# A mixture of experts behind cross attention: which freed memory the first tiles of the expert stage are put in

## The chip, the core and the metric

The kernel runs on one core of a Trainium2 chip. The metric is the device time of one execution in microseconds (us). The engines are TensorE (PE in the profile), VectorE (DVE), ScalarE (ACT), GpSimd (POOL) and SyncE (SP), which here only issues DMAs. Lines such as L1551 are lines of the kernel before.

## The reference

`x` has 16 blocks of 128 rows of 512. Attention over a small context is added to it, and then the output of a routed feed-forward layer with 32 experts, 8 of them for each row, and one shared expert:

```python
x = x + xattn(layernorm(x), ctx, ctx)
h = layernorm(x)
tidx, tw = gate(h)                       # 8 of 32 experts for each row, with weights
comb = zeros(T, 32).at[rows, tidx].set(tw)
g, u = h @ w1[e].T, h @ w3[e].T          # for each expert e
routed = sum over e of comb[:, e] * ((silu(g) * u) @ w2[e].T)
sh = (silu(h @ sw1.T) * (h @ sw3.T)) @ sw2.T
x = x + routed + sh
```

## The kernel before

**Stages.** Attention comes first (to about 105 us), then the routing (`route`, `slot_tokens`: which row goes to which slot of which expert), to about 183 us. Beside the routing and for some 28 us after it TensorE works on the shared expert. Its last step is `shared_down` (L1381): two matmuls per block of 128 rows fill a PSUM bank `y`, and `add_down` (L1395) has VectorE add `y` to the block `xs[b]` (here called the sum of x; L1396) and SP write the block to `out` (L1397). From about 211 us on the 32 experts follow one after another, each in two pieces of at most 352 rows.

**An expert's work.** `gather` fetches the rows of 128 slots (POOL issues it), `transpose` (VectorE) and `block_copies` (small copies, most on ScalarE, some on VectorE, L1506) turn them into `xall`, whose parts are called `half`. The first and the last expert go through `direct` and `up` (L1533): a matmul with w1, silu on ScalarE into a tile `sg` (L1551), a matmul with w3, and a product on VectorE into `sa` (L1555). All others go through `seven` (L1624), which forms the up-projection of two halves with seven products instead of eight. It needs sums of quarters of the weights (`weight_sums`, L1563: four VectorE instructions s1, s2, a21 in place, s4, all at L1574) and of the tokens (`token_sums`, L1592: t1, t2, b12 in place, t4, at L1603). Its first product is copied by ScalarE from PSUM into a tile `p1` (L1661), and VectorE adds further products to it, in tiles `u2` and `z` (L1622). `down` (L1740) multiplies `sa` with the expert's w2, `evict` (L1763) scales the result by the routing's weight into a tile `yw` on ScalarE, and `send` scatters it with adding into `out` (POOL, L1721).

**Order.** The instructions of TensorE, VectorE, ScalarE and POOL stand in the order in which the program text issues them; no scheduler moves them. `soon(f)` puts an evacuation one step later. Within the experts' loop, side work (`on_DVE`, `on_ACT`: sums, transposes, copies) is dealt out over the steps of a piece by a count of its cost. Weight sums for expert k+1 are issued in the first piece of expert k, token sums for k+1 in its second.

**Memory.** Tiles come from pools. When a pool is closed, later pools may take its memory, and the first instruction that writes there waits for all that last used it. Two such changes of hands matter:

- `early` holds the routing's tiles. It is closed at L1424, and `tp` (L1427) is opened behind it. `tp` holds `own`, `blocks` and, in the kernel before, `yw` (4 tiles of 2 KiB per partition).
- `x_only` holds the rows of x (`xs`). It is closed at L1814, after the last sums of x have been issued, and `late` (L1815) takes its memory. `late` holds `sg` (3 tiles of 2 KiB), `s1`, `s2`, `s4` (2 each of 2 KiB), `t1`, `t2`, `t4`, `p1`, `u2` and `z`.

The loop that issues the last eight blocks of the shared expert reads as follows (`products` holds the sum of x):

```python
for i, b in enumerate(downs):            # L1806
    shared_down(b, ps_p)
    transpose_to(min(6 + i, last_slice(3)))
    ...                                  # some copies into xall
    for f in products:
        f()
    products.clear()
x_only.close()                           # L1814
late = ctx.enter_context(tc.tile_pool(name="late", bufs=2, side="right"))
```

Of the kernel before, what the change touches and what calls it, by code (L numbers as in the profile page):

```python
# [9 lines left out]
F32 = mybir.dt.float32  # L10
# [8 lines left out]
P = 128  # L19
# [27 lines left out]
def tile_xattn_moe(  # L47
# [16 lines left out]
    B, S, D = x.shape  # L64
# [5 lines left out]
    TB = 512  # L70
# [981 lines left out]
    def experts(ups, in_order, later, products):  # L1052
# [374 lines left out]
        tp = ctx.enter_context(tc.tile_pool(name="tp", bufs=2))  # L1427
# [15 lines left out]
        def experts_at(j):  # L1443

            for k in range(E):
                a, b = max(begins[k], j * P), min(begins[k + 1], (j + 1) * P)
                if a < b:
                    yield k, a - j * P, b - j * P, a - begins[k]
# [5 lines left out]
        xg, yws = {}, {}  # L1454
# [75 lines left out]
        def soon(f, after=1):  # L1530
            jobs.setdefault(now + after, []).append(f)

        def up(n, i, w, banks):  # L1533

            k, first, end = pieces[n]
            m = min(end, begins[k] + ROOM[ORDER[k]]) - first
            act = acts_of[k % NA][:, :, first - begins[k] : first - begins[k] + m]

            acc = banks[w] = ps_p.tile([P, TB], F32, tag="p", name="gu")
            for d in range(ND):  # L1540
                nc.tensor.matmul(
                    acc[:, 0:m],
                    lhsT=wup[k % NW][:, w, d, ts(i, P)],
                    rhs=half[n % NH][:, d, 0:m],
                    start=(d == 0),
                    stop=(d == ND - 1),
                )
            if w == 0:
                sl = late.tile([P, 2, M], F32, tag="sg", name="sg", bufs=3)
                sl = banks[2] = sl.rearrange("p a b -> p (a b)")  # L1550
                soon(lambda: nc.scalar.activation(sl[:, 0:m], acc[:, 0:m], AF.Silu))  # L1551
            else:
                sl = banks[2]
                soon(
                    lambda: nc.vector.tensor_tensor(  # L1555
                        act[:, i, :], sl[:, 0:m], acc[:, 0:m], ALU.mult
                    )
                )

        M = TB // 2  # L1560
        sums = {}

        def weight_sums(k):  # L1563


            a11, a12, a21, a22 = (
                wup[k % NW][:, :, d : d + 2, ts(i, P)] for i in range(2) for d in (0, 2)
            )
            s1, s2, s4 = (
                late.tile([P, 2, 2, P], F32, tag=name, name=name) for name in ("s1", "s2", "s4")  # L1570
            )
            sums[k] = s1, s2, a21, s4
            return [
                lambda o=o, a=a, b=b, op=op: nc.vector.tensor_tensor(o, a, b, op)  # L1574
                for o, a, b, op in (
                    (s1, a21, a22, ALU.add),
                    (s2, s1, a11, ALU.subtract),
                    (a21, a11, a21, ALU.subtract),
                    (s4, a12, s2, ALU.subtract),
                )  # L1580
            ]

        def halves_of(k):

            h = ROOM[ORDER[k]] // 2
            return [
                half[n % NH][:, d : d + 2, 0:h] for d in (0, 2) for n in (2 * k, 2 * k + 1)
            ]
# [32 lines left out]
        def add(out_, a, b):  # L1621
            soon(lambda: nc.vector.tensor_tensor(out_, a, b, ALU.add))  # L1622

        def seven(k):  # L1624


            h = ROOM[ORDER[k]] // 2
            act = acts_of[k % NA]
            a11, a12, _, a22 = (
                wup[k % NW][:, :, d : d + 2, ts(i, P)] for i in range(2) for d in (0, 2)  # L1630
            )
            s1, s2, s3, s4 = sums[k]
            b11, _, b21, b22 = halves_of(k)
            t1, t2, t3, t4 = tsums.pop(k)
            both = 2 * h <= TB
            size = M if both else HM

            def new(name, n, size, bufs=2):
                t = late.tile([P, 4 * M if name == "z" else TB], F32, tag=name, name=name, bufs=bufs)
                return t[:, 0 : n * size].rearrange("p (n t) -> p n t", n=n)[:, :, 0:h]  # L1640

            def silu(to, of, after):
                soon(lambda: nc.scalar.activation(to, of, AF.Silu), after)

            def times(to, a, b, after):
                soon(lambda: nc.vector.tensor_tensor(to, a, b, ALU.mult), after)

            act0, act1 = act[:, 0, 0:h], act[:, 1, 0:h]
            act2 = act[:, :, h : 2 * h]

            for w in (slice(0, 2),) if both else (slice(0, 1), slice(1, 2)):

                many = w.stop - w.start

                def bank():
                    p = ps_p.tile([P, TB], F32, tag="p", name="p")
                    return p[:, 0 : many * size].rearrange("p (n t) -> p n t", n=many)[:, :, 0:h]

                pa, p1 = bank(), new("p1", many, size, 1)
                product(pa, a11[:, w], b11)  # L1660
                soon(lambda p1=p1, pa=pa: nc.scalar.copy(p1, pa))  # L1661
                yield
                pb, u2 = bank(), new("u2", many, size)
                product(pb, s2[:, w], t2)
                add(u2, p1, pb)
                yield
                pc = bank()
                z = new("z", 2 * many, size)
                z0, z1 = z[:, 0:many], z[:, many : 2 * many]
                product(pc, s1[:, w], t1)  # L1670
                add(z1, u2, pc)
                yield
                pd = bank()
                product(pd, s3[:, w], t3)
                add(z1, z1, pd)
                yield
                product(pa, a12[:, w], b21, first=False)
                if both:
                    sl = new("sg", 1, TB, 3)[:, 0]
                    silu(sl, pa[:, 0], 1)  # L1680
                    times(act0, sl, pa[:, 1], 2)
                elif w.start == 0:
                    silu(act0, pa[:, 0], 1)
                else:
                    times(act0, act0, pa[:, 0], 1)
                yield
                product(pc, s4[:, w], b22, first=False)
                add(z0, u2, pc)
                if both:
                    sl = new("sg", 2, M, 3)  # L1690
                    silu(sl, z[:, 0::2], 2)
                    times(act2, sl, z[:, 1::2], 3)
                elif w.start == 0:
                    silu(act2, z, 2)
                else:
                    times(act2, act2, z, 2)
                yield
                product(pd, a22[:, w], t4, first=False)
                add(u2, u2, pd)
                if both:  # L1700
                    sl = new("sg", 1, TB, 3)[:, 0]
                    silu(sl, u2[:, 0], 2)
                    times(act1, sl, u2[:, 1], 3)
                elif w.start == 0:
                    silu(act1, u2[:, 0], 2)
                else:
                    times(act1, act1, u2[:, 0], 2)
                yield
# [52 lines left out]
            soon(lambda: evict(j, y))  # L1761

        def evict(j, y):  # L1763
            yws[j] = tp.tile([P, D], F32, tag="yw", name="yw", bufs=4)
            nc.scalar.activation(yws[j], y, AF.Copy, scale=wt[:, j : j + 1])  # L1765
            for args in waiting:
                send(*args)
            waiting.clear()
            rows_of = {k: (a, b) for k, a, b, _ in experts_at(j)}
            ks = sorted(rows_of)  # L1770
            send(j, ks[0], *rows_of[ks[0]])
            waiting.extend((j, k, *rows_of[k]) for k in ks[1:])
# [33 lines left out]
        for i, b in enumerate(downs):  # L1806
            shared_down(b, ps_p)
            transpose_to(min(6 + i, last_slice(3)))
            for f in copies[len(copies) * i // len(downs) : len(copies) * (i + 1) // len(downs)]:
                f()  # L1810
            for f in products:
                f()
            products.clear()
        x_only.close()  # L1814
        late = ctx.enter_context(tc.tile_pool(name="late", bufs=2, side="right"))  # L1815
        KEPT = 2

        def fast(k):
            return 0 < k < E - 1
# [14 lines left out]
        for n in range(len(pieces)):  # L1834
            k = pieces[n][0]
            odd = n % 2
# [8 lines left out]
                steps = 4  # L1845

            on_DVE, on_ACT = [], []
            if not odd and fast(k + 1):
                on_DVE += [(4, f) for f in weight_sums(k + 1)]
            to_turn = last_slice(min(n + 4, last_piece))  # L1850
            turning = [(5, lambda j=j: transpose(j)) for j in range(n_turned, to_turn)]
# [29 lines left out]
            for step in range(steps):  # L1881
# [3 lines left out]
                for i, (side, total) in enumerate(sides):  # L1885
                    due = done / sum(dues)
                    while side and lefts[i] > total * (1 - due) + 0.01:
                        c, f = side.pop(0)
# [97 lines left out]
```

## Time and profile before

| what | value |
|---|---|
| median of 3 runs | 879.42 us (879.39 to 880.23) |
| profiled execution: time, and its span from first to last instruction | 881.58 us, 879.7 us |
| granted TensorE clock, mean | 0.998 |
| TensorE busy, 211 to 225 us / 225 to 240 / 240 to 255 | 14.00 / 11.08 / 15.00 us |
| ScalarE busy in the same | 8.03 / 14.46 / 14.53 us |
| VectorE busy in the same | 10.65 / 13.09 / 13.16 us |
| TensorE busy in each stage of 60 us from 300 to 840 | 60.00 us |

The first three columns of time are the last step of the shared expert's sums with expert 0 (211 to 225), the first half of expert 1 (225 to 240) and what follows. A busy figure of a stage cannot tell what the stage waits for; for that the waits, the chain of waits and the timeline of each engine are read. A row of the waits has the engine and line that waited, what it waited for, the total in us, how often, and the longest. A row of a timeline has start, length, engine, line, operation, output and inputs, shapes and count, and in brackets the idle time before it and what ended it.

### The profile page before, as it was taken

Reading aid. Unit: us, or ns where it says so; the run is one execution under the profiler, and the core shown is the slowest. Engines: PE = TensorE matmul, PEld = TensorE weight load, DVE = VectorE, ACT = ScalarE, POOL = GpSimd, SP = SyncE. Lnnn points to the kernel's source line nnn. Section 1 sums busy time; section 2 is a strip of 40 time slices with the busy share of each in tenths; the row PEclk is TensorE's granted clock in tenths of the full one; section 3 lists DMA queues with packets and bytes.
Section 4 is the critical chain, followed back from the end, with each engine's and each line's share of the span. In section 5 each row is a group of like instructions: output and inputs, shape, how many; then the busy total and the mean of one; then the engine's idle time right before and its main releaser. Section 6 shows DMA issues by size and latency. Waiting matters only on the chain.

```text
span 879.7 us, 13628 instructions
## 1 busy us (share of the span) xinstructions
PE 861.7 (98%) x4015; PEld 538.5 (61%) x4015; DVE 625.9 (71%) x1599; ACT 689.4 (78%) x1570; POOL 476.4 (54%) x590
## 2 busy tenths in 40 slices
PE   8999999999899999999999999999999999999995
PEld 5344444546565665666666666676767777777763
DVE  7877778846976777777777777776867777777510
ACT  5888732537998898888898989898898899999831
POOL 4487550053355576656556666565556656554454
PEclk9999999999999999999999999999999999999999
DMA  9111112556377788778778787877778888786544
GB/s 307 58 48 50 49 50 77 211 156 197 110 169 162 172 202 191 177 169 182 165 181 184 192 188 191 186 210 175 187 158 206 195 176 178 197 190 122 88 76 54
DMA packets 59876, 137.15 MB, mean 156 GB/s; under 512 B 12168, under 2 KB 16392, under 8 KB 59792
## 3 DMA queue, kind: packets, MB, share of 16 engines
q0 software_dynamic: 32032, 69.25, 41.9%
q1 hardware_dynamic: 27680, 66.81, 22.1%
q8 instruction: 34, 0.56, 0.3%
q14 instruction: 50, 0.41, 0.2%
q10 hardware_dynamic: 80, 0.13, 0.0%
HBM read 96.71 MB, written 46.73 MB: 163 GB/s over the span
## 4 chain that ended last, share of the span: by engine, by line
PE 88%; POOL 3%; ACT 3%; issue 2%; DVE 2%; DMA 2%; POOLq 0%; ACTq 0%
PE p L1612 42%; PE y L1749 24%; PE gu L282 6%; PE sc L489 5%; PE oT L505 4%; PE x L459 2%; PE y L1386 2%; POOL out_dram L1721 2%; ACT xall L1506 2%; DMA out_dram<-yw,token 1%; PE tok L1038 1%; DVE x L1396 1%; PE lgT L566 0%; PE lg L581 0%; DVE xall L1506 0%
## 5 line engine op out<-in xcount | busy, mean ns | idle before, releaser
L1506 ACT COPY xall<-blocks 32x256 f32<-32x256 f32 (+10 forms) x1137 | 418.9, 368 | 15.0
L1721 POOL DMA_INDIRECT out_dram<-yw,token x150 | 246.2, 1641 | 212.0 <-ACT yw L1765 79.7
L1749 PE MATMUL y<-wdn,sa 128*128 128x512 f32 (+2 forms) x672 | 259.1, 594 | 0.0
L1460 POOL DMA_INDIRECT xgs<-rows,token x138 | 150.7, 1092 | 134.5 <-DVE token L1050 53.2
L1612 PE MATMUL p<-xall,wup 128*128 128x270 f32 (+27 forms) x720 | 185.6, 394 | 2.0 <-ACT p L1661 2.0
L1612 PEld LDWEIGHTS p<-xall,wup 128*128 128x128 f32 x720 | 136.5, 190 | 46.6 <-issue 16.1
L1749 PEld LDWEIGHTS y<-wdn,sa 128*128 128x128 f32 (+2 forms) x672 | 100.9, 171 | 83.7 <-issue 72.2
L1765 ACT ACTIVATE yw<-y,wt 128x512 f32<-128x512 f32 x138 | 94.7, 686 | 70.6 <-PE y L1749 39.4
L1612 PE MATMUL p<-t,s 128*128 128x270 f32 (+27 forms) x480 | 125.7, 394 | 1.1 <-DVE t L1603 1.1
L1612 PEld LDWEIGHTS p<-t,s 128*128 128x128 f32 x480 | 91.0, 190 | 39.0 <-issue 22.4
L1509 DVE STREAM_TRANSPOSE blocks<-xgs 128x512 f32<-128x512 f32 x138 | 97.5, 706 | 0.2
L1622 DVE TENSOR_TENSOR z<-u,p 128x270 f32<-128x270 f32 (+27 forms) x96 | 48.8, 509 | 68.5 <-PE p L1612 63.3
L499 ACT ACTIVATE p<-sc 128x1024 f32<-128x1024 f32 x64 | 62.1, 1023 | 13.6 <-PE sc L489 13.6
L1612 PE MATMUL p<-t,wup 128*128 128x270 f32 (+27 forms) x240 | 63.8, 396 | 0.7 <-DVE z L1622 0.7
L1612 PE MATMUL p<-xall,s 128*128 128x270 f32 (+27 forms) x240 | 63.6, 396 | 0.5 <-DVE z L1622 0.4
L1612 PEld LDWEIGHTS p<-t,wup 128*128 128x128 f32 x240 | 45.0, 190 | 25.9 <-issue 14.1
L282 PE MATMUL gu<-xall,sup 128*128 128x512 f32 x128 | 59.2, 601 | 0.0
L1622 DVE TENSOR_TENSOR u<-u,p 128x270 f32<-128x270 f32 (+27 forms) x48 | 24.4, 509 | 44.9 <-PE p L1612 36.9
L1612 PEld LDWEIGHTS p<-xall,s 128*128 128x128 f32 x240 | 45.2, 190 | 16.9 <-issue 4.3
L1506 DVE COPY xall<-blocks 32x256 f32<-32x256 f32 (+11 forms) x187 | 51.3, 299 | 3.5
L489 PE MATMUL sc<-qT,kz 32*128 32x512 f32 x256 | 44.2, 639 | 0.5 <-DVE qT L480 0.2
L1603 DVE TENSOR_TENSOR t<-xall,t 128x540 f32<-128x540 f32 (+27 forms) x60 | 43.3, 722 | 0.5
(218 smaller groups left out, 916.2 us busy)
## 6 DMA issues: line engine op xcount, KB each, us to landing
wup<-in_w_dram SPq DMA_DIRECT2D x64, 512.0 KB
wdn<-in_w_dram SPq DMA_DIRECT2D x32, 512.0 KB
rows<-xn SPq DMA_DIRECT2D x16, 256.0 KB
out_dram<-x SPq DMA_DIRECT2D x16, 256.0 KB
x<-in_x_dram SPq DMA_DIRECT2D x15, 256.0 KB
out_dram<-yw,token POOLq DMA_INDIRECT x150
xgs<-rows,token POOLq DMA_INDIRECT x138
cTs<-in_cT_dram SPq DMA_DIRECT2D x4, 256.0 KB
```

What stands on the lines that cost most here:

```text
L282: nc.tensor.matmul(acc, lhsT=sup[:, w, d, ts(i, P)], rhs=xnT[k][:, d, :], start=(d == 0), stop=(d == ND - 1),)
L489: nc.tensor.matmul(scs[j // 2][:, j % 2], lhsT=kzs[b // 4 % 2][rows, b % 4, i, :], rhs=qT[rows], start=True, stop=True, tile_position=(j * ...
L499: nc.scalar.activation(p, sc, AF.Exp, scale=1.0 / HD**0.5)
L1460: nc.gpsimd.indirect_dma_start(out=t, out_offset=None, in_=rows[:, :], in_offset=bass.IndirectOffsetOnAxis(ap=token[:, j : j + 1], axis=0) ...
L1506: yield on_ACT, 1 + many, lambda dst=dst, of=of, copy=copy: copy(dst, of)
L1509: nc.vector.transpose(blocks[:, j % NB_BUF, :], xgs[:, j % NG_BUF, 0:D])
L1603: yield lambda o=out_, a=a, b=b: nc.vector.tensor_tensor(o, a, b, ALU.subtract)
L1612: nc.tensor.matmul(acc[:, i, 0:h], lhsT=w[:, i, d, :], rhs=x[:, d, :], start=(first and i == d == 0), stop=(i == outs[-1] and d == 1), ski ...
L1622: soon(lambda: nc.vector.tensor_tensor(out_, a, b, ALU.add))
L1721: ins = nc.gpsimd.indirect_dma_start(out=flat, out_offset=bass.IndirectOffsetOnAxis(ap=token2[:, k - 1 : k] if a else token[0:b, j : j + 1 ...
L1749: nc.tensor.matmul(y[c0:c1, :], lhsT=acts_of[k % NA][:, i, col : col + c1 - c0], rhs=wdn[k % NW][:, i, :], start=(i == 0), stop=(i == NI - 1),
L1765: nc.scalar.activation(yws[j], y, AF.Copy, scale=wt[:, j : j + 1])
```

## The change

It has four parts. The tiles `sg` are taken from `tp` instead of `late`, both in `up` and in `seven`, and so are `s1`, `s2` and `s4`. The tiles `yw` go the other way, from `tp` to `late`. The weight sums of expert 1 are issued in the loop over the last blocks of the shared expert, in its first pass, ahead of the sum of x; the experts' loop leaves them out for its first piece. The number of instructions on each engine stays the same, and no size changes.

```diff
@@ up
             if w == 0:
-                sl = late.tile([P, 2, M], F32, tag="sg", name="sg", bufs=3)
-                sl = banks[2] = sl.rearrange("p a b -> p (a b)")
+                sl = banks[2] = tp.tile([P, TB], F32, tag="sg", name="sg", bufs=3)
                 soon(lambda: nc.scalar.activation(sl[:, 0:m], acc[:, 0:m], AF.Silu))
@@ weight_sums
             s1, s2, s4 = (
-                late.tile([P, 2, 2, P], F32, tag=name, name=name) for name in ("s1", "s2", "s4")
+                tp.tile([P, 2, 2, P], F32, tag=name, name=name) for name in ("s1", "s2", "s4")
             )
@@ seven
             def new(name, n, size, bufs=2):
-                t = late.tile([P, 4 * M if name == "z" else TB], F32, tag=name, name=name, bufs=bufs)
+                pool = tp if name == "sg" else late
+                t = pool.tile([P, 4 * M if name == "z" else TB], F32, tag=name, name=name, bufs=bufs)
@@ evict
-            yws[j] = tp.tile([P, D], F32, tag="yw", name="yw", bufs=4)
+            yws[j] = late.tile([P, D], F32, tag="yw", name="yw", bufs=4)
@@ the loop over the last blocks of the shared expert
-            for f in products:
+            for f in (weight_sums(1) if i == 0 else []) + products:
                 f()
             products.clear()
@@ the experts' loop
-            if not odd and fast(k + 1):
+            if not odd and k and fast(k + 1):
                 on_DVE += [(4, f) for f in weight_sums(k + 1)]
```

## The prediction

> **What bounds the kernel now.** I read the page first, then the waits of the stretch from 205 to 246 us, the chain of waits there, and the order of TensorE's and VectorE's instructions in time. TensorE is busy nearly all the time and carries the chain, so only time in which TensorE stands still can be won.
>
> ```profile
> PE 861.7 (98%) x4015; PEld 538.5 (61%) x4015; DVE 625.9 (71%) x1599; ACT 689.4 (78%) x1570; POOL 476.4 (54%) x590
> PE 88%; POOL 3%; ACT 3%; issue 2%; DVE 2%; DMA 2%; POOLq 0%; ACTq 0%
> ```
>
> The change touches two waits, both on the write-outs of x. They are the first two lines here; the last three are TensorE's own waits a little later:
>
> ```profile
> ACT sg L1551 <- DMA out_dram<-x: 5.7, 1, 5.7
> DVE s L1574 <- DMA out_dram<-x: 3.0, 1, 3.0
> PE p L1612 <- ACT p L1661: 2.0, 1, 2.0
> PE p L1612 <- DVE t L1603: 1.1, 1, 1.1
> PE p L1612 <- DVE z L1622: 0.7, 1, 0.7
> ```
>
> A wait of ScalarE costs nothing by itself. The chain (start, length, what) shows that this one does:
>
> ```profile
> 214.97 0.70 DVE x L1396
> 215.69 2.85 DMA out_dram<-x
> 218.65 0.38 ACT sg L1551
> ...
> 234.36 0.46 ACT p L1661
> 234.84 0.52 DVE u L1622
> ...
> 237.29 0.71 DVE blocks L1509
> 238.14 0.45 DVE z L1622
> 238.63 6.18 PE p L1612 x20
> ```
>
> From the last sum of x the chain goes through its transfer to the first silu. ScalarE then works without a pause (copies into xall, silus) until the copy of p at 234.36, VectorE follows, and TensorE is let go at 238.63. So 5.7 us of waiting on ScalarE reach TensorE 16 us later. What they cost is read from TensorE's starts (start, busy, operation):
>
> ```profile
> 227.36 2.63 PE L1612 MATMUL p<-t,s 128*128 128x352 f32 x8 [1.09 <-DVE t L1603]
> 229.83 1.35 PE L1612 MATMUL p<-xall,wup 128*128 128x352 f32 x4
> 231.02 1.88 PE L1749 MATMUL y<-wdn,sa 128*128 128x512 f32 x4
> 234.86 1.45 PE L1612 MATMUL p<-xall,wup 128*128 128x352 f32 x4 [1.97 <-ACT p L1661]
> 236.46 1.45 PE L1612 MATMUL p<-xall,s 128*128 128x352 f32 x4
> 238.63 1.45 PE L1612 MATMUL p<-t,wup 128*128 128x352 f32 x4 [0.73 <-DVE z L1622]
> 239.92 1.35 PE L1612 MATMUL p<-xall,wup 128*128 128x352 f32 x4
> 241.10 2.53 PE L1612 MATMUL p<-t,s 128*128 128x352 f32 x8
> ```
>
> These are the seven products of expert 1's first half, which begin at 224.93. One product takes 1.18 us from start to start (239.92 to 241.10), a group of y 1.72 (chain). Seven and one y: 7 x 1.18 + 1.72 = 9.98 us. The round takes 239.92 - 224.93 = 14.99. **So 5.0 us are lost here**; the three listed waits add up to only 3.8, because they are counted from modelled ends of matmuls.
>
> **What the Trainium skill says.** Perfetto Trace Analysis, section "Tensor Engine Instruction (MATMUL, LD_WEIGHTS)": TensorE's end times are an estimate, and ScalarE and VectorE are strict first-in-first-out. The trace agrees with both: 5.0 us by starts against 3.8 by ends, and VectorE's matmul-independent copies stand behind its 3.0 us wait. The same page, "DMA Instruction — HWDGE (DVE, Sync)": a DMA's semaphore comes only after its write is confirmed, which can be surprisingly late for HBM; here 2.85 us pass from issue to release. VectorE: DVE Perf Modes, "The TRN2 errata": an fp32 tensor_tensor over 512 elements takes 691 ns; the trace's s rows take 681 to 693. SBUF — State Buffer, "SBUF: two separate sides": VectorE with two SBUF inputs and a GpSimd operation that reads SBUF lock each other out. The second expert's weight sums ran at 231.93 beside a gather (231.58 to 232.58) in 0.68 and 0.69 us, so I charge nothing.
>
> **The change, part by part.**
> (a) *sg from the routing's memory.* The instruction order of the changed kernel shows that the first silu waits for TensorE alone. Its matmuls are a quarter of the first piece's 7 us after 211.11, so ready at about 212.9; ScalarE's copies end at 198.91 + 14.05 = 212.96. It starts at about 213.05 instead of 218.65: **ScalarE is 5.6 us earlier.** The wait for x's eight queues moves to the first copy of p on ScalarE (p1 stays in the rows' memory), due near 228.9, when the transfers have long landed (218.54): free.
>
> (b) *Weight sums of expert 1 ahead of the last eight sums of x.* Four instructions of 0.69 us, starting about 0.6 to 0.7 apart: 2.6 us taken from the stretch after 215.7 and put behind the copies that end at 199.6. There VectorE idles now:
>
> ```profile
> 199.02 0.57 DVE L1506 COPY xall<-blocks 32x256 f32<-32x256 f32 x2
> 203.16 0.69 DVE L1396 TENSOR_TENSOR x<-y,x 128x512 f32<-128x512 f32 x1 [3.57 <-PE y L1386]
> ```
>
> 2.6 fit in 3.57. Their operands are there: the loads were issued before 153.4. Odd is that y's four matmuls (from 197.38, 0.43 apart) end near 199.1, four us before that sum starts; why its release came late the trace doesn't tell. If the release is as late again, the sums hide wholly. If it comes at once, the sums of x start at 202.2, 0.96 us earlier than now. If VectorE stops for the 3.57 us whatever is queued, everything behind comes 2.6 us later. I take the first; -0.96 and +2.6 are the ends.
>
> (c) *VectorE after 215.66.* The 3.0 us wait goes, and 2.6 of sums: it moves to the token sums' t1, the first user of the rows' memory there. In the new order: three copies (1.1) to 216.8, transpose and own (0.8) to 217.6, product sa (0.42), transpose and own to 218.85, sa, two copies to 219.9. t1 needs ScalarE's three copies behind the second silu: 213.05 + 0.4 + 4.42 + 0.4 + 1.56 = 219.9. So t1 starts at about 219.95 instead of 225.49, over 1 us after the last landing. t2 ends at 221.8; TensorE wants it at 226.11: the 1.1 us stall is gone.
>
> (d) *TensorE's round.* With no stall its products start at 224.93, 226.11, 227.3, 228.5, y at 229.7, then 231.4 (needs p1's copy), 232.6 (needs z's first sum) and 233.7 (needs z's second). ScalarE: third silu by 222.35, nine copies (3.3), fourth silu by 226.1, seven copies (2.75), p1's copy ends at 229.35. VectorE: u at 229.4, s4 0.65, z to 230.95, copies, transpose and own, second z to 233.15. Slacks 2.0, 1.6 and 0.6 us: **all 5.0 us go.**
>
> (e) *yw into the rows' memory.* The first eviction, now at 238.23, comes 15 us after the landing; four buffers as before: nothing. SP's loads keep their order; the one for expert 4 loses a wait on VectorE that did not end last. POOL's order is unchanged; its gathers hang on VectorE's transposes, which come no later, and the scatters on evictions that move forward.
>
> (f) *Afterwards.* ScalarE has no pause over 0.1 us until 276.6, so its 5.6 us of lead stay while TensorE gains 5.0; the stall at 267.95 (0.55 by starts, 0.38 listed, behind p1's copy) can shrink by up to 0.55. I take 0.2. Later nothing holds TensorE but its own work, so the gain stands to the end.
>
> **Sum:** 5.0 + 0.2 = 5.2 us. The profiled execution had a span of 879.7 and 881.58 in all, which would be 876.4; the runs' median is 879.42, 2.2 less, so the forecast is 879.42 - 5.2 = **874.2**. Its own range is 873.5 (all of the later stall, x earlier) to 875.6 (slacks 1 us worse).
>
> **Rivals.**
> *A, the weight sums push x (2.6 us later).* ScalarE's copies from 204.76 on read transposes that start right behind a sum of x, and would stand 2.3 us; t1 would wait for a landing at 221.2 and VectorE's own queue to about 222.5. First z then ends at about 233.3 against 232.55, second at 235.5: stalls of 0.75 and 1.0, so the gain is 3.2: 876.2. For it: the odd 3.57 us. Against: the label says PE.
> *B, lost banks: slower.* The sums of x also empty y's PSUM banks. The third (10th row block) ends at 207.65, and TensorE takes its bank at 211.11; the other margins are 3.3 us or more. If the four instructions delay x by d, TensorE loses d - 3.3. To lose more than the 5.0 it needs d over 8.3; at d = 11, 882. Against: 2.6 us of work with operands that are there, so d could exceed 2.6 only by a wait nobody shows.
> *C, hardly a gain.* ScalarE's lead is eaten before p1's copy (silus waiting on TensorE, copies on transposes), or TensorE meets a later limit and gives it back: 878.5. Against: every later stage of 60 us up to 840 has TensorE busy 60.0. *The change not doing what it says* is excluded by the order: sg waits for TensorE alone.
>
> **How the numbers follow.** Forecast 0.80, A 0.10, C 0.06, B 0.04. Range 873.4 to 877.2: the forecast's ends with 0.1 below, and A with 1 us of spread above (the three runs differ by 0.84). A measurement tells about 0.2% (1.76 us, that is 877.66) from no change. Faster: forecast and A, less a little, 0.89; same 0.06; slower 0.05.
>
> **What would show it.** The first sg at about 213 with no DMA wait; the four weight sums at 199.6 and sums of x not after 203.2; t1 near 220; TensorE's first round 10 us instead of 15, with no wait on p1 or t. It is wrong if the sums of x start after 205, if p1's copy comes after 231, or if TensorE's gain at 240 is not there at 840.

## The result, and the profile after

The changed kernel takes 875.97 us (median of 6 runs, 875.87 to 876.05) beside 879.78 us for the kernel before in the same comparison (6 runs, 879.23 to 880.23). The ratio is 0.9957, with an interval of 0.9944 to 0.997: 3.81 us gained. The two profiled executions differ by more: 881.58 to 875.97, or 5.61 us. That difference of 1.8 us is what most of the experiments below turned out to be about.

First the page of the kernel after: the busy times, and the shares of the chain that ended last.

```profile
PE 860.4 (98%) x4015; PEld 539.0 (62%) x4015; DVE 625.7 (72%) x1599; ACT 689.3 (79%) x1570; POOL 478.7 (55%) x590
PE 92%; POOL 3%; issue 2%; DMA 2%; ACT 1%; DVE 0%; POOLq 0%; ACTq 0%
```

The work is the same; TensorE's share of the chain has risen from 88% to 92%, and ScalarE's and VectorE's have gone from 5% together to 1%. Then the chain from 195 to 246 us (start, length, what), where it ran before from a sum of x through a transfer to ScalarE:

```profile
197.53 13.73 PE y L1386 x32
211.27 13.81 PE gu L1541 x64
225.08 4.73 PE p L1611 x16
229.81 1.72 PE y L1749 x4
231.53 8.28 PE p L1611 x28
```

Nothing but TensorE is left in it. Of the waits from 205 to 246 us, those on the write-outs of x are gone, and no matmul of a product appears as waiting on another engine; what VectorE still waits for is ScalarE:

```profile
DVE u L1621 <- ACT p L1661: 2.5, 2, 1.6
DVE sa L1554 <- ACT sg L1550: 1.4, 2, 0.8
DVE t L1602 <- ACT xall L1506: 0.6, 1, 0.6
```

TensorE's timeline (start, busy, operation) gives what that is worth:

```profile
224.92 1.35 PE L1611 MATMUL p<-xall,wup 128*128 128x352 f32 x4
226.10 2.53 PE L1611 MATMUL p<-t,s 128*128 128x352 f32 x8
...
231.37 1.35 PE L1611 MATMUL p<-xall,wup 128*128 128x352 f32 x4
232.55 1.35 PE L1611 MATMUL p<-xall,s 128*128 128x352 f32 x4
233.73 1.35 PE L1611 MATMUL p<-t,wup 128*128 128x352 f32 x4
234.92 1.35 PE L1611 MATMUL p<-xall,wup 128*128 128x352 f32 x4
...
263.14 1.21 PE L1611 MATMUL p<-xall,s 128*128 128x280 f32 x4
```

The round, from the first product to the first of the next half, takes 234.92 - 224.92 = 10.00 us, where it took 14.99. The last line is the matmul that stood behind the later stall; before, it reads:

```profile
268.73 1.21 PE L1612 MATMUL p<-xall,s 128*128 128x280 f32 x4 [0.38 <-DVE z L1622]
```

So the lead is 5.00 us at the end of the round (239.92 - 234.92) and 5.59 behind the stall (268.73 - 263.14). It stays 5.59 to the last matmul.

### The profile page after: what moved, and what is told of

The parts are those of the page before. It is cut to its first block, busy times and chain, and to the rows that moved or that the text cites. A ratio compares the mean times of both kernels' runs of the same rounds, so it can differ in the third digit from the quotient of the medians.

```text
span 874.1 us, 13629 instructions
## 1 busy us (share of the span) xinstructions
PE 860.4 (98%) x4015; PEld 539.0 (62%) x4015; DVE 625.7 (72%) x1599; ACT 689.3 (79%) x1570; POOL 478.7 (55%) x590
## 4 chain that ended last, share of the span: by engine, by line
PE 92%; POOL 3%; issue 2%; DMA 2%; ACT 1%; DVE 0%; POOLq 0%; ACTq 0%
PE p L1611 43%; PE y L1749 24%; PE gu L282 6%; PE sc L489 5%; PE oT L505 4%; PE y L1386 3%; PE x L459 2%; POOL out_dram L1721 2%; DMA out_dram<-yw,token 2%; PE gu L1541 2%; PE tok L1038 1%; PE lgT L566 0%; PE lg L581 0%; ACT p L499 0%; PE rank L1277 0%
## 5 line engine op out<-in xcount | busy, mean ns | idle before, releaser
L1721 POOL DMA_INDIRECT out_dram<-yw,token x150 | 243.6, 1624 | 210.7 <-DMA out_dram<-yw,token 78.6
L1460 POOL DMA_INDIRECT xgs<-rows,token x138 | 155.4, 1126 | 128.1 <-DVE token L1050 53.2
L282 PE MATMUL gu<-xall,sup 128*128 128x512 f32 x128 | 59.2, 602 | 0.0
```

The source lines that it names most:

```text
L282: nc.tensor.matmul(acc, lhsT=sup[:, w, d, ts(i, P)], rhs=xnT[k][:, d, :], start=(d == 0), stop=(d == ND - 1),)
L1460: nc.gpsimd.indirect_dma_start(out=t, out_offset=None, in_=rows[:, :], in_offset=bass.IndirectOffsetOnAxis(ap=token[:, j : j + 1], axis=0) ...
L1721: ins = nc.gpsimd.indirect_dma_start(out=flat, out_offset=bass.IndirectOffsetOnAxis(ap=token2[:, k - 1 : k] if a else token[0:b, j : j + 1 ...
```

## The experiments

Two theories stood against each other on why the timed runs gain 1.8 us less than the profile, numbered here as in the expectations below. Theory 1: the late release of the first y of the last eight (VectorE's odd 3.57 us) is always there, and the gain is lost elsewhere. Theory 2: it is not the same in all executions, and the kernel before is slow where it comes late. Beside these stood the prediction's own open questions: what each half of the change is worth alone, and what a delay of the sums of x costs.

One measure is used for all. Call "y8" the start of the first matmul of L1386 for the last eight blocks, and give the start of the first following sum of x (L1396) as a distance from y8. In the profiled execution of before it was 203.16 - 197.38 = 5.78 us. Where VectorE does not have to wait it is 2.25 to 2.26, as the second chip will show. "The round" is again TensorE's time from the first product of expert 1 to the first product of its next half (the fourth behind the y group), 10.0 us without a stall. Every run below is timed beside the kernel before on the same chip. The first comparison was on one chip, and the three batches on three others. Each chip was used in one batch only, so what is said of a chip below may also be said of its batch.

### Second chip: the kernel before, a delay, and each half of the change

The kernel before itself, for its profile on this chip. No edit.

> The kernel before, unchanged, profiled once more. Its profiled execution of 881.58 us was 1.8 us slower than the median of its timed runs (879.78), while the changed kernel's profiled and timed executions agree (875.97). Theory 1 (the late release of the eighth block's y is always there, and the rest is scatter of the profile): the first of the last sums of x starts near 203.2 us again, the round of expert 1 takes 15.0 us, the profiled time is near 881.6. Theory 2 (in most executions the release comes earlier and the wait on x's write-outs is shorter): the sum starts between 199.6 and 202, the round takes 12 to 14 us, and the profiled time is near 879.5.

877.42 us beside 877.44 (40 runs), ratio 1.0001 [0.9993, 1.001]: on this chip the kernel before is 2.34 us faster than on the first. TensorE's and VectorE's timelines say why:

```profile
199.68 4.03 PE L1386 MATMUL y<-sdn,sa 128*128 128x512 f32 x9
```

```profile
201.32 0.58 DVE L1506 COPY xall<-blocks 32x256 f32<-32x256 f32 x2
201.93 0.69 DVE L1396 TENSOR_TENSOR x<-y,x 128x512 f32<-128x512 f32 x1
```

The sum of x follows the copies at once, 2.25 us after y8, and has no bracket with an idle time. (All starts are 2.3 us later in this execution, most of it for a reason told at the end; distances are not touched by it.) The waits from 205 to 250 us shrink to suit, and so does the round:

```profile
DVE s L1574 <- DMA out_dram<-x: 2.4, 1, 2.4
ACT sg L1551 <- DMA out_dram<-x: 1.6, 1, 1.6
...
PE p L1612 <- DVE z L1622: 0.6, 1, 0.6
```

```profile
227.23 1.35 PE L1612 MATMUL p<-xall,wup 128*128 128x352 f32 x4
...
238.07 1.35 PE L1612 MATMUL p<-xall,wup 128*128 128x352 f32 x4
```

The silu waits 1.6 us instead of 5.7, and the round takes 238.07 - 227.23 = 10.84 us instead of 14.99. The 5.0 us that the prediction sets out to win are not there on this chip; 0.84 are. Theory 1 is ruled out here. The round is below the 12 to 14 us that Theory 2 had expected; its 879.5 us was met by the profiled execution (879.72) only because of the delay told at the end, and the median is 877.4.

The kernel before with four additions put on VectorE ahead of that sum of x. They fill the place of the weight sums, and their result is used by nothing:

```diff
+            if i == 0:
+                scratch = xnp.tile([P, D], F32, tag="xn2", name="scratch", bufs=4)
+                for _ in range(4):
+                    nc.vector.tensor_tensor(
+                        scratch.rearrange("p (w d t) -> p w d t", w=2, d=2),
+                        wup[1][:, :, 0:2, ts(1, P)], wup[1][:, :, 2:4, ts(1, P)], ALU.add)
             for f in products:
```

> The kernel before with four additional additions of 128x512 on VectorE (2.6 to 2.9 us in all, into a tile that nobody reads) where the changed kernel puts the weight sums. Theory 1 (VectorE idles 3.57 us there in every execution): covered, no change within 0.3 us of the kernel before. Theory 2 (it idles there only in some executions, the profiled one among them): the sums of x and their write-outs come later than usual, and the time rises by 1 to 2.5 us to about 881 to 882.

880.1 us, ratio 1.0032 [1.0022, 1.0042], 2.66 slower. VectorE's timeline and the waits:

```profile
199.44 2.87 DVE L1814 TENSOR_TENSOR scratch<-wup 128x512 f32<-128x512 f32 x4
202.23 0.68 DVE L1396 TENSOR_TENSOR x<-y,x 128x512 f32<-128x512 f32 x1
```

```profile
ACT sg L1551 <- DMA out_dram<-x: 4.4, 1, 4.4
...
PE p L1612 <- ACT p L1661: 2.0, 1, 2.0
```

A delay of 2.8 us made by hand (5.03 from y8 instead of 2.25) brings back the silu's long wait, TensorE's 2.0 us wait for the copy of p, and a round of 13.66 us. So no idle time hid the additions here, and late sums of x are enough to bring the loss, with no late release. The time rose by a little more than the 1 to 2.5 us expected.

The tiles alone: the changed kernel with the weight sums back in the experts' loop.

```diff
-            for f in (weight_sums(1) if i == 0 else []) + products:
+            for f in products:
-            if not odd and k and fast(k + 1):
+            if not odd and fast(k + 1):
```

> The tiles change memory as in the change, but the weight sums of expert 1 stay behind the last sums of x. Main theory (ScalarE's wait is what costs, the weight sums then hold VectorE 2.6 us too long): first silu at 213.05 us, t1 near 222.5, second sum of z at 234.2 instead of 232.5, one stall of about 1.0 us before the last product, round 11.1 us, time 877.0. Rival (the place of the weight sums doesn't matter once nothing waits for x): 876.0. Rival (VectorE's queue is what counts): 878 to 879.

875.81 us, ratio 0.9981 [0.9974, 0.9987]. 877.0 was missed; the rival's 876.0 came within 0.2. The sum of x starts 2.26 us after y8, the round is 10.0 us, and 1.63 us are gained: the 0.84 of the round, and by the traces 0.43 at the later stall. The other 0.36 are not placed; the profiled execution, with 876.2 us, lies 0.39 above its median, so they are not in the traces. On this chip the second half of the change isn't needed.

The weight sums alone: the changed kernel with `sg` back in the rows' memory.

```diff
-                sl = banks[2] = tp.tile([P, TB], F32, tag="sg", name="sg", bufs=3)
+                sl = banks[2] = late.tile([P, TB], F32, tag="sg", name="sg", bufs=3)
-                pool = tp if name == "sg" else late
+                pool = late
```

> Only s1, s2, s4 change memory and the weight sums of expert 1 go ahead of the last sums of x; sg stays in the memory of the rows of x. Main theory: the first silu waits for the last write-out until about 217.7, p1's copy comes at 233.5, round about 14 us, time about 879.9, as good as no gain over the kernel before. Rival (VectorE's part is worth its share of 2.6 of 5.6): about 878.

880.21 us, ratio 1.0031 [1.002, 1.0041]: 2.77 **slower**. The time, the wait and the round (14.05 us) came near what was expected; that this is slower than the kernel before, and not level with it, was not:

```profile
ACT sg L1550 <- DMA out_dram<-x: 4.5, 1, 4.5
...
PE p L1611 <- ACT p L1661: 2.0, 1, 2.0
```

The four weight sums stand ahead of the sum of x and push it to 4.77 us from y8, and `sg` still waits for the last write-out. It is the hand-made delay over again, with useful instructions in its place. This run moves the tiles of the weight sums and their place together, so it does not show what freeing VectorE's wait alone would do.

### Third chip: the changed kernel, one tile alone, and the rivals' delays

The changed kernel, unedited:

> The change itself, once more, beside the kernel before. In the last comparison the kernel before took 877.44 us and not 879.78. Theory 2 (the kernel before depends on when y's release reaches VectorE, the changed kernel doesn't): the changed kernel takes 875.8 to 876.1 again, whatever the kernel before does, so that the gain is 1.4 to 1.7 us where the kernel before takes 877.4 and 3.8 where it takes 879.8. Theory 1 (the gain is a fixed 3.8 to 5.6 us, only the level differs): the changed kernel is near 873.6 where the kernel before is at 877.4.

876.03 us beside 881.17 (19 runs), ratio 0.9946 [0.9933, 0.996]: a gain of 5.14 us, because the kernel before is slower here than on any other chip and the changed one is the same to 0.1 us. The first sum of x starts 5.88 us after y8, with 1.0 us of idle time left behind the weight sums; the round is 10.0 us. Here the case that (b) of the prediction took is what happened: the weight sums are hidden wholly.

Only `sg` moved (with `yw` in exchange): as the tiles alone, and `s1`, `s2`, `s4` back in the rows' memory.

```diff
-                tp.tile([P, 2, 2, P], F32, tag=name, name=name) for name in ("s1", "s2", "s4")
+                late.tile([P, 2, 2, P], F32, tag=name, name=name) for name in ("s1", "s2", "s4")
```

> Only sg (and yw in exchange) changes memory; s1, s2, s4 stay in the memory of the rows of x and the weight sums of expert 1 stay behind the last sums of x. With sums of x from 199.7 on: the last landing at 214.5 lets the weight sums start at 214.6, p1's copy comes at 228.85, second sum of z ends near 233.5 against a need at 233.7: no stall, 875.8 to 876.0, so sg alone is the whole gain. Rival (both waits must go together): a stall of 1 us or more is left, 877.0 or more.

880.1 us, ratio 0.9989 [0.9981, 0.9997]: 1.07 of the 5.14 us. 875.8 to 876.0, which took a prompt release for granted, was missed by over 4 us; the rival, that both waits must go together, was met. VectorE's timeline first, then the waits from 205 to 250 us:

```profile
203.01 0.69 DVE L1396 TENSOR_TENSOR x<-y,x 128x512 f32<-128x512 f32 x1 [3.54 <-PE y L1386]
```

```profile
ACT xall L1506 <- DVE blocks L1509: 4.3, 1, 4.3
DVE s L1573 <- DMA out_dram<-x: 2.8, 1, 2.8
...
PE p L1611 <- ACT p L1661: 0.9, 1, 0.9
PE p L1611 <- DVE t L1602: 0.8, 1, 0.8
PE p L1611 <- DVE z L1621: 0.7, 1, 0.7
```

The idle time is back on this chip, and `sg` no longer waits. But VectorE stands at the first weight sum until x has landed, the transposes behind it are late, and ScalarE waits 4.3 us for them before its next copies. It is rid of one wait and gets another of nearly the same end; the round takes 13.64 us. The two waits stand side by side on two engines, and with a late release VectorE's alone is almost enough to hold the round up.

The changed kernel with the same four additions, put ahead of the weight sums and so ahead of the sum of x; rival A of the prediction, made by force:

> The changed kernel with four additional additions of 128x512 on VectorE (2.9 us, into a tile nobody reads) ahead of the weight sums, so that the sums of x start near 205.1 instead of 202.2. It is the prediction's rival A, forced. ScalarE's copies stand about 2 us behind late transposes, the second sum of z ends near 234.8: stalls of 1.2 to 1.8 us, 877.1 to 877.8. Rival (VectorE's remaining pauses, 2.8 us in all, absorb it): 876.0.

877.43 us, ratio 0.9965 [0.9953, 0.9977]: 1.40 over the unedited kernel on this chip, as expected. The sum of x starts 7.57 us after y8, 1.7 later than without the additions, since they use up the idle 1.0 first.

```profile
ACT xall L1506 <- DVE blocks L1509: 1.6, 1, 1.6
...
PE p L1611 <- DVE z L1621: 0.6, 1, 0.6
```

ScalarE's copies wait for the transposes behind the sums of x, and TensorE loses 0.86 us at the second z (round 10.86) and 0.6 later. There is no wait on a DMA in it.

The same with twelve additions instead of four; rival B:

> The same with twelve additional additions (8.3 to 8.7 us): the prediction's rival B, forced. TensorE waits for the banks of y from 211 us on, about 4 us by the margins of the changed kernel's trace (4.2 us between the third sum of x and the first piece's first matmul), and 1.5 to 3 us more at the products: 881.5 to 883. If the banks don't hold TensorE, the stall is at p1 and z alone and the time 880 or less.

883.29 us, ratio 1.0031 [1.0019, 1.0043]: 7.26 over the unedited kernel, 2.12 slower than before, and 0.3 above the range expected. TensorE's timeline shows the bank:

```profile
211.40 3.78 PE L1386 MATMUL y<-sdn,sa 128*128 128x512 f32 x8 [3.67 <-DVE x L1396]
215.23 4.95 PE L1541 MATMUL gu<-xall,wup 128*128 128x256 f32 x21
```

The sum of x starts at 210.66, 13.40 us after y8, or d = 7.5 later than in the unedited kernel. TensorE stands 3.67 us for a bank of y that a sum of x has not yet emptied, and expert 0 begins 17.97 us after y8 instead of 13.73, 4.2 us late; the prediction's d - 3.3 gives 4.2. It loses another 0.3 within expert 0 (14.16 us to expert 1 instead of 13.81), 2.1 in the round (12.09) and 0.6 later, none of which the rival had charged. Together they make up the 7.26.

### Fourth chip: before, after and the parts once more

The kernel before and the changed kernel, both unedited:

> The kernel before, once more. Late release: first of the last sums of x at 203.2 us, silu at 218.7, round 15.0, later stall 0.6, time 881.2 to 881.6. Release on time: sum at 199.7, silu at 214.5, round 10.8, 877.4. If the time of y's release is not what separates the levels, the round doesn't follow it.

> The change once more: 875.8 to 876.1 and a round of 10.0 us with either release.

880.29 us beside 880.22 (33 runs), ratio 1.0001 [0.9993, 1.0009], and 876.08 us, ratio 0.9958 [0.9944, 0.9971]: 4.14 gained. VectorE's timeline and the waits of the kernel before:

```profile
204.36 0.69 DVE L1396 TENSOR_TENSOR x<-y,x 128x512 f32<-128x512 f32 x1 [2.68 <-PE y L1386]
```

```profile
ACT sg L1551 <- DMA out_dram<-x: 4.6, 1, 4.6
```

The sum of x starts 4.92 us after y8, after 2.68 us of idle time; the silu waits 4.6, and the round takes 14.18 us. The release, the round and the time lie between the two cases expected, and the round follows the release. In the changed kernel the weight sums lie in that idle time, and the round is 10.0, as expected.

The tiles alone, as on the second chip:

> The tiles change memory, the weight sums of expert 1 stay behind the last sums of x, once more, because chips differ in when the first of the last eight y is released to VectorE. Where the release is late (5.8 us after that y's first matmul): the sums of x start at 203.2, the weight sums end at 218.3, one stall of about 1 us is left before the seventh product, round 11.0 us, time 877.0, so moving the weight sums is worth 1 us. Where it is on time (1.9 us after): no stall, round 10.0, 875.8, and moving them is worth nothing. Rival: 875.8 on both.

876.47 us, ratio 0.9959 [0.9945, 0.9973]: 0.4 over the changed kernel, where 0.9 was expected. In the profiled execution, which took 877.44 us, the sum of x is late (5.64 us from y8), and

```profile
ACT xall L1506 <- DVE blocks L1509: 1.3, 1, 1.3
...
PE p L1611 <- DVE z L1621: 0.4, 1, 0.4
```

show how the four weight sums, back in VectorE's later queue, now make the transposes late; the round is 10.66 us, and 0.6 more are lost at the later stall. The four other executions took 876.35 to 876.69 us, about 0.9 less than the profiled one; that the release came earlier in them is likely, but not shown. So the second half of the change is worth about 0.4 us in the runs on this chip, and some 1.3 us in the one execution with the later release.

Only `sg` moved, as on the third chip:

> Only sg changes memory, once more. Late release: round 13.6 as before on such a chip, 880.1. Release on time: no stall, 875.8 to 876.0.

879.21 us, ratio 0.9987 [0.9981, 0.9994]: 1.01 gained. The sum of x is 4.95 us from y8, ScalarE's copies wait 3.3 us for the transposes, and the round is 12.61 us: the same pattern as on the third chip, 1.0 us milder, with a release that is 0.8 us earlier. The 13.6 us and 880.1 expected were those of the third chip's later release.

### What the chips say together

Medians in us; in brackets the difference from the kernel before on the same chip. The second column is the first sum of x after y8 in profiled executions whose queue has nothing put ahead of it.

| chip | y8 to x | before | after | tiles only | sg only | weight sums only |
|---|---|---|---|---|---|---|
| second | 2.25, 2.26 | 877.44 | | 875.81 (-1.63) | | 880.21 (+2.77) |
| first | 5.78 | 879.78 | 875.97 (-3.81) | | | |
| fourth | 4.92, 4.95, 5.64 | 880.22 | 876.08 (-4.14) | 876.47 (-3.75) | 879.21 (-1.01) | |
| third | 5.76 | 881.17 | 876.03 (-5.14) | | 880.10 (-1.07) | |

The changed kernel is the same on three chips to 0.11 us; the kernel before spreads over 3.7 us. From the second chip to the fourth the sums of x come 2.7 us later (4.92 against 2.25) and the kernel before takes 2.78 more; the hand-made delay of 2.8 us cost 2.66. About one us lost for each us that the sums of x are late: that is the rate of the kernel before, and Theory 2 holds. Theory 1 falls, since the gain isn't lost anywhere: it isn't there to be had where the release is prompt.

Left open: why y is released late on some chips and not on others. The fourth chip's 4.92 and 5.64 show that it varies on one chip too, though these are traces of two kernels. On the first chip only one execution of before has a trace, 5.78 us; that its timed runs were released earlier is inferred from their shorter time. It fits that in the one trace of the changed kernel there TensorE's report of the first y comes 4.86 us after y8. The changed kernel itself was not run on the second chip, nor `sg` alone there, nor the weight sums alone on a chip with the late release.

## Why the prediction was right, and where it was not

The forecast of 874.2 us was 1.8 us too low; the range of 873.4 to 877.2 holds the result, though the forecast's own range, to 875.6, ends 0.4 short of it: the wider range, drawn for rival A, saved it. It was luck, too, that the comparison ran on a chip with the late release; on the second chip, judging by the tiles alone, the gain would have been some 1.6 us.

**The mechanism, (a) to (e), was right to about a tenth of a us.** From ScalarE's and VectorE's timelines of the kernel after:

```profile
213.03 0.38 ACT L1550 ACTIVATE sg<-gu 128x256 f32<-128x256 f32 x1
```

```profile
199.62 0.69 DVE L1573 TENSOR_TENSOR s<-wup 128x512 f32<-128x512 f32 x1
...
201.55 0.68 DVE L1573 TENSOR_TENSOR s<-wup,s 128x512 f32<-128x512 f32 x1
202.25 0.69 DVE L1396 TENSOR_TENSOR x<-y,x 128x512 f32<-128x512 f32 x1
...
219.87 0.89 DVE L1602 TENSOR_TENSOR t<-xall 128x704 f32<-128x704 f32 x1 [0.55 <-ACT xall L1506]
```

The first silu was put at 213.05 and starts at 213.03, with no wait for a DMA. The weight sums were put behind 199.6 and start at 199.62. t1 was put at 219.95 and starts at 219.87, and as (c) says it is ScalarE's copies that end last there. The first copy of p starts at 228.75 and ends at 229.20 (229.35 was predicted), and the two z end at 230.79 and 232.97 (230.95 and 233.15). The round fell by 4.99 us where 5.0 were charged. For (b), the sums of x start at 202.25 with no idle time before them, 0.9 us earlier than before, where the case that was taken had 203.2. It looks like the case called "at once", but is not: TensorE's report of the first y comes at 202.23, 4.86 us after y8 (its event stands in the trace), and the weight sums happen to end at the same moment. The release was late again, only less so.

**(f) was mis-sized.** 0.2 us was taken for the later stall; TensorE's lead grew by 0.59 (5.00 to 5.59). ScalarE kept its lead and the whole stall went, the upper end that the step had named.

**The step that failed is the last one of the sum**, "the runs' median is 879.42, 2.2 less, so the forecast is 879.42 - 5.2". It carries a gain read from one profiled execution over to other executions as if both differed by a constant. From profile to profile the kernel gained 5.61 us, 0.4 more than the 5.2 of the sum; from median to median 3.81. The wait that was removed had its length from a release that the prediction itself called odd, and left unexplained in (b). The experiments show that just this release varies (the sum of x starts 2.25 to 5.78 us from y8), and that before's time follows it about one to one, while after's does not. Had the 2.2 us been read as a sign that the profiled execution had more of the removed wait than the timed ones, the forecast would have been near 876.4, the figure that the sum gave for the profiled execution.

**Rival A** was right in its mechanism: the transposes behind the sums of x, then ScalarE's copies, then the z. Forced with 1.7 us it cost 1.40. **Rival B** had the bank right: 4.2 us for d = 7.5, as its formula gives. But it charged nothing for expert 0 and the products behind it, and so put the turning point at d = 8.3; at 7.5 the kernel is already 2.12 us slower than before. **Rival C** and the case that nothing changes found no support: the lead at 263 us is there at the end.

**What it did not ask** is what each half is worth. The two waits on x run side by side on ScalarE and VectorE. To free ScalarE's alone gave 1.0 us on both chips where it was tried; to free both gave 3.75 on the fourth; the earlier weight sums add 0.4 there, and without the move of `sg` cost 2.77 on the second chip, by making the write-outs late for which `sg` still waits.

The prediction's use of the Trainium skill, Perfetto Trace Analysis, section "DMA Instruction — HWDGE (DVE, Sync)", that a write's semaphore comes only when the write is confirmed, fits every kernel that kept the wait: from the issue behind the last sum of x to the landing it took 2.2 to 2.9 us. With the tiles elsewhere no wait for it is left in the changed kernel.

## What to carry to other kernels

A wait for freed memory can be held by several engines at once; list every first writer of that memory and look at what remains when one of them is moved: here one alone gave a fifth to a quarter of the gain. When a profiled execution is slower than the runs, ask whether the wait to be removed is longer in it; a gain read from one trace is worth no more than that wait is in the ordinary execution. A change that adds slack to a place where timing varies can make the time the same wherever it runs, as on the three chips here; its gain then depends on how bad the kernel before is on the chip at hand.

## What the runs showed that had not been expected

**TensorE's report that a result is complete is not a fixed time.** With the same instructions, the sum of x starts 2.25 us after the first matmul of its bank on one chip, with no idle time, and 4.9 to 5.9 us after it on three others, where VectorE stands idle for 2.7 to 3.6 us (1.0 behind the weight sums) and the trace names TensorE as the releaser. The traces also hold the events of the semaphore by which TensorE reports a finished y. On the second chip (the tiles alone) those of the first three y come 1.9, 3.6 and 5.3 us after y8, each 0.6 us after the start of its last matmul. In the kernel before on the first chip the matmuls keep the same pace, but the three events come bunched, 5.76, 5.84 and 5.90 us after y8; on the fourth chip 4.90, 5.69 and 5.75. The fourth y is then reported 0.6 us after its last matmul starts, as usual. So neither the matmuls nor VectorE are late, but the reports of three results, held up and then delivered together. What holds them up is open. Semaphore events are missing in the traces of just these chips (678 of TensorE's are recorded in the first chip's trace of before, 730 in the second chip's); whether the recording has a part in the delay isn't shown.

**Short drops of TensorE's clock, whatever the kernel.** In some executions the matmuls at 121 to 124 us run slower. From the windows of the changed kernel on the fourth chip (stretch; length, then busy time and count of TensorE, its loads, VectorE, ScalarE, GpSimd; granted clock; DMA share and GB/s), and the same window on the first chip:

```profile
120.70:124.10 3.40, 3.40 (x5) 1.35 (x4) 2.54 (x8) 1.98 (x3) 3.38 (x7) 0.50 0.01 2
```

```profile
120.70:124.10 3.40, 3.40 (x9) 1.51 (x8) 2.68 (x9) 2.43 (x3) 3.40 (x8) 1.00 0.01 2
```

The clock is halved for 3.4 us, four matmuls come 0.85 us apart instead of 0.43, and everything behind is 1.7 us later, half of the 3.4 (from the matmuls of L282 that start at 120.35 us to y8 it takes 78.89 us; on the first chip, from 120.17, 77.20). It makes up most of the 2.3 us by which the starts in the second chip's trace of before are late, and adds 1.76 us to the profiled execution here (877.84 us against the median of 876.08). On the second chip 6 of 40 runs of before lie over 1.2 us above their median. Their mean granted clock is 0.994 to 0.995 and that of the other 34 is 0.996 to 0.997, so it is likely that they have it; only profiled executions show it for certain.

In two traces such a drop also falls into the round, just behind TensorE's 1.97 us wait for the copy of p: in the kernel before on the fourth chip, and in the weight sums alone on the second (from 234.2 us there).

```profile
236.50:239.90 3.40, 3.40 (x7) 1.88 (x6) 3.34 (x9) 3.25 (x11) 0.54 (x1) 0.50 0.00 0
```

It lengthens these two rounds, 14.18 and 14.05 us, by about 0.3 us: from the end of the wait to the end of the round they take 5.35 us, where the hand-made delay, with the same wait and no drop, takes 5.06. The later stall is 0.3 us shorter in return. The same wait brings no drop in the first chip's trace of before; what decides it isn't shown.
